# Half units for small experts, loads of the sums past a branch, and an ordered fill in a two-layer decoder with routed experts

## The chip, the cores and the metric

The kernel runs on one core of a Trainium2 chip, as one program. The metric is the device time of one execution in microseconds (us). Times shown are medians of plain runs; beside them stands one execution taken by the hardware profiler, whose records are called the trace. The engines are TensorE (PE for its matmuls, PEld for its weight loads), VectorE (DVE), ScalarE (ACT), GpSimd (POOL) and SyncE (SP), which only issues transfers here.

## What is computed

The input is `x`, 32 sequences of 100 tokens with 256 features (3200 tokens), and a context of 361 tokens with 128 features for each sequence. Six blocks follow each other, each added to its own input:

```python
x = x + _L0_attn_ref(_layernorm(x), ...)    # causal attention, 16 heads of 64
x = x + _L0_xattn_ref(_layernorm(x), ctx)   # cross attention, 16 heads of 16
x = x + _L0_ffn_ref(_layernorm(x), ...)     # 8 experts, 2 for each token, and a shared one
x = x + _L1_attn_ref(_layernorm(x), ...)    # 16 heads of 16, masked scores, no softmax
x = x + _L1_xattn_ref(_layernorm(x), ctx)   # cross attention, 16 heads of 64
x = x + _L1_ffn_ref(_layernorm(x), ...)     # 64 experts, 8 for each token, and a shared one
```

In the last block each token picks 8 of 64 experts, and an expert takes at most its first 256 tokens (`CAP`):

```python
xe = jnp.zeros((E, CAP, H)).at[sorted_e, pos].set(tok_sorted, mode='drop')
h = jax.nn.silu(jnp.einsum('ech,efh->ecf', xe, w1)) * jnp.einsum('ech,efh->ecf', xe, w3)
ye = jnp.einsum('ecf,ehf->ech', h, w2)
out = jax.ops.segment_sum(vals * flat_w[:, None], flat_t, num_segments=T)
shared = jax.nn.silu(x @ shared_gate.T) * (x @ shared_up.T) @ shared_down.T
return out + shared
```

All data is float32. With the given inputs the router uses 31 of the 64 experts, and 23 of these receive more than 128 tokens (this was worked out from the reference's routing, not from the trace).

## The kernel before, in words

The tokens lie as 25 tiles of 128 rows (`NF`), `x` stays in the on-chip memory throughout, and `xnT` holds the normed, transposed rows. The blocks run one after the other. Three things set the order of work. TensorE's order is written out by hand: inside `tc.manual_schedule` its instructions run as the program text issues them. On the other engines the framework's planner places each instruction by its inputs and its own estimate of costs, and each engine then runs its list in order, so one that waits holds those behind it. `depend` (L1696) adds an edge by hand. Lastly there are limited buffers, above all the eight PSUM banks.

**Start of layer 1's attention (`l1_attn`, L920 to L1098).** The results of layer 0's experts lie in memory as `y_d`. `gather0` (L1249) fetches the two rows that belong to each token of a tile by two indirect transfers on GpSimd (L1255, into buffers `yk`, eight of them) and adds each to `x` on VectorE (L1260). `norm_stats` (L165) takes the statistics; with the last tile of its group it adds epsilon (L182), takes the square root on ScalarE (L183) and the reciprocal on VectorE (L184). `norm_rows` then scales the rows (L187), and `norm_turn` transposes them on TensorE (L209). The groups are 4 tiles, then 3 each (`FRONT1`). `ahead` fills TensorE meanwhile with keys (`keys1`, L761) and values (`vals1`, L771) of the next block, whose inputs don't depend on `x`. Each product must be copied out of its bank by `evac` (L126), which sends every second copy to ScalarE (L130) and the rest to VectorE (L131). Before, statistics of the first four tiles stand ahead of the fill; then come four key groups (eight products) and three value halves (nine products), the turns of the first group, a fifth key group, the projections, then a fourth value half and the second group. The loop over the 32 sequences gathers the tiles of the group after next in its first three steps out of four and turns a group in the fourth; these gathers' adds have no added edge.

**Routing (`route`, `list1`, `tick`).** During the cross attention of layer 1 the router scatters each token's row, its number and its weights into `x1_d`, 256 places for each expert (L1647). `list1` (L1658) counts the rows of each expert, and lists those in use in the order of their numbers; an unused place in the list holds a dummy.

**Layer 1's experts (`l1_ffn`, L1704; `units`, L1786).** 18 pieces' worth of the shared expert run first on TensorE. A flag on GpSimd (L1760) waits for the last scattered row. Then `units` takes the first 32 listed experts, one a unit with all 256 places: `weights` (SyncE, L1794) nine units ahead, `rows` (SyncE, L1800) five ahead, `expert_turn` (transposes, L1838; copy on ScalarE, L1842), one step later `expert_hidden` (gate and up, Silu L1854, product L1856), and another step later `expert_add`: the down product, its weighting on VectorE (L1875, three buffers `ye`) and for each half of 128 rows a scatter-add on GpSimd (L1879) into one of two arrays `sum_d`, odd and even units apart. Each scatter-add waits for those of the unit two before. `room` mixes the rest of the shared expert in, at 0.9 us of it a unit from the first unit on. A branch runs units for the other 32 places if more than 32 experts are in use. At the end, SyncE loads both sums in ten transfers (L1780), VectorE adds them (L1782) and ScalarE's queue stores the output (L1783).

Of the kernel before, what the change touches and what calls it, by code (L numbers as in the profile page):

```python
# [9 lines left out]
F32 = mybir.dt.float32  # L10
# [41 lines left out]
UNITS, MORE = 32, 32  # L52
# [27 lines left out]
class Kernel:  # L80
    def __init__(self, ctx, tc, a):
# [6 lines left out]
        self.norms, self.norm_of = {}, {}  # L88
# [76 lines left out]
    def norm_stats(self, f, groups, after=None):  # L165
# [15 lines left out]
        if i == n - 1:  # L181
            nc.vector.tensor_scalar_add(rstd, mv[:, :, 1], EPS)  # L182
            nc.scalar.activation(rstd, rstd, AF.Sqrt)  # L183
            nc.vector.reciprocal(rstd, rstd)  # L184
# [576 lines left out]
    def keys1(self, n):  # L761

        b, g = divmod(n, 4)
        t = self.k1[n] = self.kv.tile([P, 2, L], F32, tag="kT", name="kT", bufs=5)
        for j in range(2):
            c = 2 * g + j
            pm = self.bank_p()[:, :L]
            self.mm(pm, [(self.w1x[1][:, c * P : (c + 1) * P], self.ctx1[b][:, :L])])
            self.evac(t[:, j, :], pm)

    def vals1(self, b, half, c):  # L771
# [7 lines left out]
        self.evac(t[:, c, :], pm)  # L779

    def l1_xattn(self):
        nc, tc, a = self.nc, self.tc, self.a
        self.route_begin()
        with ExitStack() as st:
# [100 lines left out]
            lay = Lay()  # L885
            self.xattn_stream(lay)
# [33 lines left out]
    def l1_attn(self):  # L920
        nc, tc, a = self.nc, self.tc, self.a
        with ExitStack() as st:
# [4 lines left out]
            for f in range(FRONT1[0]):  # L927
                self.gather0(pool, f)
                self.norm_stats(f, FRONT1)
# [111 lines left out]

            halves = deque((b, half) for b in range(2) for half in range(2))

            def ahead(steps, n):
                for i in steps:
                    self.keys1(i)
                for _ in range(n):
                    b, half = halves.popleft()
                    for c in range(NKC):
                        self.vals1(b, half, c)  # L1050

            with tc.manual_schedule(engines={mybir.EngineType.PE}):
                for i in range(2):
                    for f in group(i):
                        if i > 0:
                            self.gather0(pool, f, self.last_row)
                            self.norm_stats(f, FRONT1)
                    f = group(i)[0]
                    if i == 0:
                        ahead(range(4), 3)  # L1060
                    else:
                        ahead([], 1)
                    turn(f, 2)
                    turn(f + 2, len(group(i)) - 2)
                    if i == 0:
                        ahead(range(4, 5), 0)
# [4 lines left out]
                for b in range(NB + 2):  # L1071
# [12 lines left out]
                    if b0 + 8 < NB:  # L1084
                        fs = group(b0 // 4 + 2)
                        if i < 3:
                            self.gather0(pool, fs[i])
# [570 lines left out]
    def list1(self, counts):  # L1658

        nc, rp = self.nc, self.rp  # L1660
        ps = self.bank_t()[:E1, :2]
        self.mm(ps[:, 0:1], [(counts, self.ones1[:, 0:1])])
        used = rp.tile([E1, 2], F32, tag="used", name="used")
        nc.vector.tensor_single_scalar(used[:, 0:1], ps[:, 0:1], 0.0, op=ALU.is_gt)
        yield 1
        self.mm(ps[:, 1:2], [(self.before1[:E1, :E1], used[:, 0:1])])
        nc.vector.tensor_copy(used[:, 1:2], ps[:, 1:2])
        at = rp.tile([E1, E1], F32, tag="at1", name="at1")
        nc.vector.tensor_scalar(at, self.io1[:E1, :], used[:, 1:2], used[:, 0:1], ALU.is_equal, ALU.mult)
        yield 1  # L1670
        pl = self.bank_t()[:, : E1 + 1]
        self.mm(pl[:, :E1], [(self.row1, at)])
        self.mm(pl[:, E1:], [(self.ones1[:E1, :], used[:, 0:1])])
# [6 lines left out]
        nc.vector.tensor_copy(self.listi[:, 2 * E1 :], pl[:, E1:])  # L1680
# [23 lines left out]
    def l1_ffn(self):  # L1704
        nc, tc, a = self.nc, self.tc, self.a
        x = self.x
        with ExitStack() as st:
# [54 lines left out]
            end = self.units(ep, 0, UNITS, steps)  # L1762
            n = nc.values_load(self.listi[0:1, 2 * E1 : 2 * E1 + 1], min_val=0, max_val=E1)
            for u in range(UNITS, E1, MORE):
                with tc.If(n > u):
                    more = self.units(ep, u, u + MORE)

                    word = pool.tile([1, 1], F32, tag="word", name="word")
                    got = nc.sync.dma_start(word, self.sum_d[0][0:1, 0:1])
                    self.depend(got, [more.ins], "the units' sums")  # L1770
# [6 lines left out]
            for f in range(0, NF, 5):  # L1777
                at = slice(f, f + 5)
                for i in range(2):
                    got = nc.sync.dma_start(ends[i][:, at, :], sums[i][:, at, :])  # L1780
                    self.depend(got, [end.ins], "the last sums")
                    nc.vector.tensor_tensor(x[:, at, :], x[:, at, :], ends[i][:, at, :], ALU.add)  # L1782
# [3 lines left out]
    def units(self, pool, u0, u1, beside=iter(())):  # L1786

        nc, tc = self.nc, self.tc
        we, xes, xTs, hTs, added = {}, {}, {}, {}, {}

        def weights(u):
            we[u] = pool.tile([P, 768], F32, tag="we", name="we", bufs=12)
            e = nc.sync.value_load(self.listi[0:1, E1 + u : E1 + u + 1], min_val=0, max_val=E1 - 1)
            nc.sync.dma_start(we[u], self.a["wexp"][bass.ds(e, 1)].rearrange("o p n -> p (o n)"))  # L1794

        def rows(u):
            xes[u] = pool.tile([P, 2, XROW], F32, tag="xe", name="xe", bufs=8)
            e = nc.sync.value_load(self.listi[0:1, u : u + 1], min_val=0, max_val=E1)
            at = self.x1_d.rearrange("(e s p) d -> e p s d", p=P, s=2)[bass.ds(e, 1)]
            got = nc.sync.dma_start(xes[u], at.rearrange("o p s d -> p (o s) d"))  # L1800
            if u0 == 0:
                self.depend(got, [self.flag.ins], "all rows are in their places")

        with tc.manual_schedule(engines={mybir.EngineType.PE}):
            room = 0.0
            for u in range(u0, u0 + 9):
                weights(u)
            for u in range(u0, u0 + 5):
                rows(u)
            for u in range(u0, u1 + 2):  # L1810
                if u + 5 < u1:
                    rows(u + 5)
                if u + 9 < u1:
                    weights(u + 9)
                if u < u1:
                    self.expert_turn(pool, u, xes, xTs)
                if u0 <= u - 1 < u1:
                    self.expert_hidden(pool, u - 1, we[u - 1], xTs, hTs)

                room = room + 0.9 if u < u1 else 100.0  # L1820
                while room > 0:
                    took = next(beside, None)
                    if took is None:
                        break
                    room -= took
                if u0 <= u - 2:
                    self.expert_add(pool, u - 2, we.pop(u - 2), xes, hTs, added)
# [5 lines left out]
    def expert_turn(self, pool, e, xes, xTs):  # L1833
        nc = self.nc
        pt = self.bank_t().rearrange("p (k s) -> p k s", k=NK)
        for s in range(2):
            for k in range(NK):
                nc.tensor.transpose(  # L1838
                    pt[:, k, s * P : (s + 1) * P], xes[e][:, s, k * P : (k + 1) * P], self.ident
                )  # L1840
        xTs[e] = pool.tile([P, NK, CAP], F32, tag="xT", name="xT")
        nc.scalar.copy(xTs[e], pt)  # L1842

    def expert_hidden(self, pool, e, we, xTs, hTs):
        nc = self.nc
        xT = xTs.pop(e)
        ph = self.bank_s()
        for i in range(2):
            self.mm(
                ph[:, i * CAP : (i + 1) * CAP],  # L1850
                [(we[:, (2 * i + k) * P : (2 * i + k + 1) * P], xT[:, k, :]) for k in range(NK)],
            )
        g = pool.tile([P, CAP], F32, tag="ge", name="ge")
        nc.scalar.activation(g, ph[:, :CAP], AF.Silu)  # L1854
        hTs[e] = pool.tile([P, CAP], F32, tag="he", name="he")
        nc.vector.tensor_tensor(hTs[e], ph[:, CAP:], g, ALU.mult)  # L1856

    def expert_add(self, pool, e, we, xes, hTs, added):
        nc, tc = self.nc, self.tc
        xe, hT = xes.pop(e), hTs.pop(e)  # L1860
        py = self.bank_m()
        for s in range(2):
# [5 lines left out]
        one = pool.tile([P, 2, E1], F32, tag="one", name="one")  # L1868
        nc.vector.scalar_tensor_tensor(  # L1869
            one, self.mid(self.io1, 2), self.listf[:, e : e + 1], xe[:, :, D + 1 :], ALU.is_equal, ALU.mult  # L1870
        )
        by = pool.tile([P, 2], F32, tag="by", name="by")
        nc.vector.tensor_reduce(by, one, AX.X, ALU.add)  # L1873
        for s in range(2):
# [3 lines left out]
        for s in range(2):  # L1878
            got = nc.gpsimd.indirect_dma_start(  # L1879
                out=self.sum_d[e % 2][:, :],  # L1880
# [5 lines left out]
            tc.declare_no_dep(got.ins, group=f"y{e}", reason="other rows")  # L1886
            tc.add_to_no_dep_group(f"y{e}", got.ins)
            self.depend(got, added.get(e % 2, []), "the sums before")
            now.append(got.ins)
        added[e % 2] = now  # L1890
# [110 lines left out]
```

## Time and profile before

| what | time |
|---|---|
| median of 3 plain runs | 3189.18 us (3188.06 to 3191.41) |
| the profiled execution | 3172.84 us |
| its span, first to last instruction | 3171.2 us |
| mean granted TensorE clock | 0.982 |
| chain that ended last: DMA `sum<-ye,xe` | 2% of the span |
| VectorE idle ahead of L1260, for DMA `yk` | 18.1 us, 13 times |
| issue to landing of the `sum` transfers, min, median, max | 2.7, 5.1, 13.5 us |
| `xe` load (L1800), `we` load (L1794), KB each | 321 and 384 KB |

Rows of a timeline give the start, the duration, the engine, the source line, the operation, what is written from what, how many, and in brackets how long the engine stood before and what ended that. A row of a group gives the busy time, the mean in ns of one, and the idle time ahead. The line of a helper is shared by all its callers, so the tile's name tells the rows apart. `wA` and `wB` are weight tiles; `kT` and `v` with input `cT` are the fill's products. The end of a matmul is modelled, so the distance from start to start is the safer measure. A releaser is inferred: where the engine named had long been done, another was the cause.

### The profile page before, as it was taken

How to read it: one execution, taken by the hardware profiler on the slowest of the kernel's cores; microseconds unless marked ns; L12 is line 12 of the kernel's file. 1: busy time of each engine (PE TensorE's matmuls, PEld its weight loads, DVE VectorE, ACT ScalarE, POOL GpSimd, SP SyncE). 2: the span in 40 equal slices, each digit the busy share in tenths (PEclk: the TensorE clock that was granted, in tenths of full speed). 3: DMA queues.
4: the chain of work that ended last, by engine and by line, in shares of the span. 5: the costliest groups of instructions: out<-in, count | busy, mean ns of one | idle time of the engine just before them, and what ended most of it. 6: DMA issues, size and time to landing. Idle time of an engine off the chain costs nothing. (4 is left out here: it accounts for less than half of the span.)

```text
span 3171.2 us, 68007 instructions
## 1 busy us (share of the span) xinstructions
PE 3053.4 (96%) x26832; PEld 2227.2 (70%) x26832; DVE 1823.4 (57%) x4697; ACT 1397.7 (44%) x4350; POOL 927.3 (29%) x1048
## 2 busy tenths in 40 slices
PE   8999999999999999999997999999999999999993
PEld 6777777566666657888884677777777777776672
DVE  6665665566676642222226776666676666666453
ACT  5555555566656521222222225545555555455220
POOL 3222212455555443000006330011212112122474
PEclk9999999999999999999998999999999999999996
DMA  8850000000000033544552000010000000000387
GB/s 310 298 201 1 1 1 1 18 14 14 13 13 14 5 112 108 198 181 176 194 201 80 12 5 6 6 33 25 22 12 10 12 8 15 7 11 5 110 213 182
DMA packets 130105, 225.86 MB, mean 71 GB/s; under 512 B 40526, under 2 KB 108422, under 8 KB 122993
## 3 DMA queue, kind: packets, MB, share of 16 engines
q1 hardware_dynamic: 98704, 127.32, 12.5%
q0 software_dynamic: 27792, 90.81, 8.8%
q8 instruction: 215, 3.52, 0.5%
q10 hardware_dynamic: 3280, 3.28, 0.3%
q14 instruction: 114, 0.93, 0.1%
HBM read 153.77 MB, written 113.61 MB: 84 GB/s over the span
## 5 line engine op out<-in xcount | busy, mean ns | idle before, releaser
L1647 POOL DMA_INDIRECT x_d<-xr,slot x200 | 194.4, 972 | 766.3 <-DVE kT L131 241.9
L442 ACT ACTIVATE wBx<-ps_t,m 100x361 f32<-100x361 f32 x512 | 281.2, 561 | 257.7 <-DVE m L439 232.1
L612 DVE TENSOR_REDUCE m<-ps_t 100x1 f32<-100x361 f32 x512 | 240.1, 525 | 113.8 <-PE ps_t L136 113.1
L136 PE MATMUL ps_t<-xnT,wA 128*128 128x200 f32 x1536 | 299.7, 340 | 2.3 <-DMA wA<-in_wq 1.7
L439 DVE TENSOR_REDUCE m<-ps_t 100x1 f32<-100x361 f32 x512 | 241.2, 526 | 79.8 <-PE ps_t L136 76.2
L136 PEld LDWEIGHTS ps_t<-xnT,wA 128*128 128x128 f32 x1536 | 259.1, 191 | 37.8 <-issue 19.9
L136 PE MATMUL ps_t<-xT,w 128*128 128x256 f32 x1276 | 283.2, 381 | 0.7 <-ACT xT L130 0.7
L136 PEld LDWEIGHTS ps_t<-xT,w 128*128 128x128 f32 x1276 | 240.0, 190 | 41.7 <-issue 9.3
L336 POOL TENSOR_TENSOR e<-e,rz 100x400 f32<-100x400 f32 x128 | 109.5, 856 | 407.7 <-DVE rz L335 398.1
L332 ACT ACTIVATE e<-s,m 100x100 f32<-100x100 f32 x512 | 186.1, 364 | 21.4 <-DVE m L326 20.7
L136 PE MATMUL ps_t<-wA,cT 128*121 128x512 f32 x384 | 187.4, 598 | 6.6 <-DVE kT L131 5.9
L633 ACT ACTIVATE e<-ps_t 121x300 f32<-121x300 f32 x512 | 173.4, 431 | 41.7 <-PE ps_t L136 41.6
L136 PE MATMUL ps_t<-cT,wA 128*128 128x361 f32 x512 | 189.9, 495 | 1.3 <-ACTq L1246 1.3
L136 PE MATMUL ps_t<-kT,qT 64*100 64x361 f32 x1024 | 189.2, 485 | 0.9 <-ACT wBx L442 0.9
L451 PEld LDWEIGHTS ps_t<-ident,wBx 100*121 100x121 f32 x1536 | 177.8, 186 | 12.3 <-ACT wBx L442 4.8
L637 POOL TENSOR_TENSOR es<-e 121x400 f32<-121x400 f32 x128 | 132.8, 1037 | 179.8 <-ACT e L633 179.6
L136 PE MATMUL ps_t<-wA,zT 128*128 128x256 f32 x800 | 185.2, 385 | 0.0
L451 PE MATMUL ps_t<-ident,wBx 100*121 100x100 f32 x1536 | 184.9, 269 | 0.0
L1328 DVE TENSOR_TENSOR h<-ps_t,g 128x256 f32<-128x256 f32 x145 | 61.2, 424 | 199.4 <-ACT g L1327 199.4
L136 PEld LDWEIGHTS ps_t<-wA,zT 128*128 128x128 f32 x800 | 150.8, 191 | 28.2 <-ACT wBx L442 3.2
L131 DVE COPY eT<-ps_t 121x300 f32<-121x300 f32 x339 | 146.7, 461 | 30.7 <-PE ps_t L451 26.7
L469 PE MATMUL ps_z<-eT,v 121*64 121x100 f32 x3072 | 160.8, 254 | 0.0
(301 smaller groups left out, 5791.7 us busy)
## 6 DMA issues: line engine op xcount, KB each, us to landing
x_d<-fill SPq DMA_DIRECT2D x16, 1284.0 KB, 22.1
we<-in_wexp SPq DMA_DIRECT2D x32, 384.0 KB, 4.5
cT<-in_ctxT SPq DMA_DIRECT2D x64, 181.5 KB, 2.3
xe<-x_d SPq DMA_DIRECT2D x32, 321.0 KB, 4.2
xe_d<-zero SPq DMA_DIRECT2D x8, 1024.0 KB, 12.9
xe<-xe_d SPq DMA_DIRECT2D x29, 256.0 KB, 2.7
y_d<-y SPq DMA_DIRECT2D x29, 256.0 KB, 8.7
sum<-fill SPq DMA_DIRECT2D x10, 640.0 KB, 9.3
```

The lines of the kernel that those rows point to most:

```text
L131: return self.nc.vector.tensor_copy(out, in_)
L136: self.nc.tensor.matmul(out, lhsT=l, rhs=r, start=(i == 0), stop=(i == n - 1))
L332: nc.scalar.activation(t[:, i, :], s[:, i, :], AF.Exp, bias=m[:, i : i + 1], accum_out=rz[:, i : i + 1])
L336: nc.gpsimd.tensor_tensor(t[:, h, :], t[:, h, :], self.last(rz[:, h], T), ALU.mult)
L439: lay.after = nc.vector.tensor_reduce(m, ps[i], AX.X, ALU.max, negate=True)
L442: nc.scalar.activation(t[:, :L], ps[i], AF.Exp, bias=m, accum_out=sums[b][:, h : h + 1])
L451: nc.tensor.transpose(pt[:, c, :], e[n, i][:, c * KC : (c + 1) * KC], self.ident[:T, :T])
L469: nc.tensor.matmul(out, lhsT=v, rhs=eT[n, i][:, c, :], start=first, stop=last)
L612: nc.vector.tensor_reduce(m[:, j, o : o + 1], ps[r], AX.X, ALU.max, negate=True)
L633: nc.scalar.activation(t[:, r], ps[r].rearrange("p (c t) -> p c t", c=NKC), AF.Exp)
L637: nc.gpsimd.tensor_tensor(s, t[:, :, 0, :], t[:, :, 1, :], ALU.add)
L1647: got = nc.gpsimd.indirect_dma_start(out=self.x1_d[:, :], out_offset=bass.IndirectOffsetOnAxis(ap=slot[:, j, k : k + 1], axis=0), in_=xr[: ...
```

## The change

It has four parts. In `list1` the experts in use are listed in two classes: those with more than 128 rows first, then those with 1 to 128. The units become 24 whole ones and 8 of the first 128 places alone; the branch now covers the second halves of those eight and all other places, and is entered if more than 24 experts have over 128 rows or more than 32 are in use. The loads of the sums at the end are declared free of the scatter-adds inside the branch. The shared expert's remaining steps are mixed in from the fourth unit on, at 1.0 a unit. In the attention's start, all five key groups and four value halves come ahead of the first tiles' statistics, with every copy on ScalarE and the first square root behind the last copy; the adds of later gathers stand behind the rows normed last.

```diff
-UNITS, MORE = 32, 32
+WHOLE, HALF = 24, 8
+UNITS = WHOLE + HALF
...
-            nc.scalar.activation(rstd, rstd, AF.Sqrt)
+            got = nc.scalar.activation(rstd, rstd, AF.Sqrt)
+            if self.norm_after is not None:
+                self.depend(got, [self.norm_after.ins], "behind the fill's copies")
...
-            self.evac(t[:, j, :], pm)
+            self.evac(t[:, j, :], pm, self.ahead_of)
...
-        self.evac(t[:, c, :], pm)
+        return self.evac(t[:, c, :], pm, self.ahead_of)
...
+            self.ahead_of = 2
             self.xattn_stream(lay)
...
             for f in range(FRONT1[0]):
                 self.gather0(pool, f)
-                self.norm_stats(f, FRONT1)
...
+            self.ahead_of = 1
             halves = deque((b, half) for b in range(2) for half in range(2))
...
+                    if i == 0:
+                        self.norm_after = ahead(range(5), 4)
+                        for f in group(0):
+                            self.norm_stats(f, FRONT1)
+                        self.norm_after = None
                     f = group(i)[0]
-                    if i == 0:
-                        ahead(range(4), 3)
-                    else:
-                        ahead([], 1)
                     turn(f, 2)
                     turn(f + 2, len(group(i)) - 2)
-                    if i == 0:
-                        ahead(range(4, 5), 0)
...
                         if i < 3:
-                            self.gather0(pool, fs[i])
+                            self.gather0(pool, fs[i], self.last_row)
...
         nc.vector.tensor_single_scalar(used[:, 0:1], ps[:, 0:1], 0.0, op=ALU.is_gt)
+        nc.vector.tensor_single_scalar(used[:, 1:2], ps[:, 0:1], float(P), op=ALU.is_gt)
+        nc.vector.tensor_tensor(used[:, 2:3], used[:, 0:1], used[:, 1:2], ALU.subtract)
         yield 1
-        self.mm(ps[:, 1:2], [(self.before1[:E1, :E1], used[:, 0:1])])
-        nc.vector.tensor_copy(used[:, 1:2], ps[:, 1:2])
+        self.mm(ps[:, 1:3], [(self.before1[:E1, :E1], used[:, 1:3])])
+        self.mm(ps[:, 3:4], [(self.ones1[:E1, :E1], used[:, 1:2])])
+        place = rp.tile([E1, 4], F32, tag="place", name="place")
+        nc.vector.tensor_copy(place, ps)
+        nc.vector.tensor_tensor(place[:, 2:3], place[:, 2:3], place[:, 3:4], ALU.add)
+        nc.vector.tensor_tensor(place[:, 1:3], place[:, 1:3], used[:, 1:3], ALU.mult)
+        nc.vector.tensor_tensor(place[:, 0:1], place[:, 1:2], place[:, 2:3], ALU.add)
...
+        nc.vector.tensor_scalar(left[:, 0:1], pl[:, E1 : E1 + 1], float(-UNITS), 0.0, ALU.add, ALU.max)
+        nc.vector.tensor_scalar(left[:, 1:2], pl[:, E1 + 1 :], float(-WHOLE), None, ALU.add)
+        nc.vector.tensor_tensor(left[:, 0:1], left[:, 0:1], left[:, 1:2], ALU.max)
...
-            end = self.units(ep, 0, UNITS, steps)
+            whole, first, second = (0, 1), (0,), (1,)
+            units = [(u, whole) for u in range(WHOLE)] + [(u, first) for u in range(WHOLE, UNITS)]
+            end = self.units(ep, units, steps)
             n = nc.values_load(self.listi[0:1, 2 * E1 : 2 * E1 + 1], min_val=0, max_val=E1)
-            for u in range(UNITS, E1, MORE):
-                with tc.If(n > u):
-                    more = self.units(ep, u, u + MORE)
...
+            with tc.If(n > 0):
+                units = [(u, second) for u in range(WHOLE, UNITS)] + [(u, whole) for u in range(UNITS, E1)]
+                more = self.units(ep, units)
...
                     got = nc.sync.dma_start(ends[i][:, at, :], sums[i][:, at, :])
                     self.depend(got, [end.ins], "the last sums")
+                    tc.declare_no_dep(got.ins, group="behind", reason="SyncE has waited in the branch")
...
+            if len(halves) == 2:
+                at = self.x1_d.rearrange("(e s p) d -> e p s d", p=P, s=2)[bass.ds(e, 1)]
+                got = nc.sync.dma_start(t, at.rearrange("o p s d -> p (o s) d"))
+            else:
+                at = self.x1_d.rearrange("(e s p) d -> s e p d", p=P, s=2)[halves[0]][bass.ds(e, 1)]
+                got = nc.sync.dma_start(t[:, 0, :], at.rearrange("o p d -> p (o d)"))
...
-                room = room + 0.9 if u < u1 else 100.0
...
+                if beside and i > 2:
+                    room = room + 1.0 if i < n_all else 100.0
+                    while room > 0:
+                        took = next(beside, None)
+                        if took is None:
+                            break
+                        room -= took
...
+            group = f"y{u}_{halves[0]}"
+            tc.declare_no_dep(got.ins, group=group, reason="other rows")
+            tc.add_to_no_dep_group(group, got.ins)
+            self.depend(got, added.get(i % 2, []), "the sums before")
             now.append(got.ins)
-        added[e % 2] = now
+            if not beside:
+
+                tc.add_to_no_dep_group("behind", got.ins)
+        added[i % 2] = now
```

`expert_turn`, `expert_hidden` and `expert_add` take the number of halves and work on 128 or 256 columns accordingly; nothing else in them changes.

## The prediction, made before the changed kernel ran

> **What bounds the kernel now.** First the page, for the whole span.
>
> ```profile
> PE 3053.4 (96%) x26832; PEld 2227.2 (70%) x26832; DVE 1823.4 (57%) x4697; ACT 1397.7 (44%) x4350; POOL 927.3 (29%) x1048
> PEclk9999999999999999999998999999999999999996
> ```
>
> TensorE is busy for 96% of 3171.2 us. So an edit pays only where TensorE has holes, runs at a lowered clock, or has already finished. The slices show two such places, around two thirds and at the end. I asked for the stretches there (length, then busy time of PE, PEld, DVE, ACT and POOL, granted clock, DMA share, GB/s).
>
> ```profile
> 1671.00:1715.00 44.00, 29.70 (x74) 14.82 (x75) 24.40 (x65) 11.36 (x21) 30.40 (x31) 0.77 0.30 87
> 1715.00:1760.00 45.00, 38.13 (x461) 24.81 (x460) 40.33 (x118) 8.92 (x23) 32.57 (x33) 0.96 0.25 73
> 1760.00:1892.00 132.00, 131.29 (x2003) 91.78 (x2001) 97.14 (x253) 36.75 (x96) 43.34 (x50) 1.00 0.01 2
> 3006.00:3098.00 92.00, 87.44 (x449) 74.60 (x448) 48.51 (x128) 25.00 (x52) 68.26 (x45) 1.00 0.83 199
> 3098.00:3136.00 38.00, 19.20 (x88) 14.22 (x87) 13.13 (x36) 4.65 (x10) 30.91 (x21) 0.80 0.59 90
> ```
>
> The start of layer 1's attention (1671 to 1760) leaves TensorE idle for 14.3 + 6.9 = 21 us. Its clock falls to 0.77 there, so some busy time is slow as well. The timeline of the fill names the cause.
>
> ```profile
> 1688.66 3.77 PE L136 MATMUL ps_t<-wA,cT 128*121 128x512 f32 x4 [5.66 <-DVE kT L131]
> 1699.37 1.23 PE L209 MATMUL ps_t<-ident,xn 128*128 128x128 f32 x4 [6.93 <-DVE xn L187]
> ...
> 1681.93 1.28 ACT L183 ACT_TABLE_LOAD   x1
> 1690.22 0.20 ACT L183 ACTIVATE rstd<-rstd 128x4 f32<-128x4 f32 x1 [7.01 <-DVE rstd L182]
> ...
> 1696.82 0.48 DVE L1260 SCALAR_TENSOR_TENSOR x_sb<-yk,wA,x_sb 128x256 f32<-128x256 f32 x1 [6.04 <-DMA yk<-y_d,wA]
> 1698.63 0.17 DVE L184 RECIPROCAL rstd<-rstd 128x4 f32<-128x4 f32 x1
> ```
>
> These are two faults of order. ScalarE stands in the square root for 7.0 us with bank copies queued behind it, and VectorE's copies queue behind adds that wait for gathers, so TensorE runs out of PSUM banks (5.66 us). Then the reciprocal for the first tiles, whose root was ready at 1690.4, stands until 1698.63 behind an add of later tiles that waits 6.04 us for its gather.
>
> In the units stage the scatter-adds on GpSimd carry the end. The group of that line, the timeline of first and last, and the wait list of VectorE:
>
> ```profile
> L1879 POOL DMA_INDIRECT sum<-ye,xe x64 | 99.2, 1550 | 44.4 <-DVE ye L1875 29.0 <-issue 9.9 <-DVE he L1856 1.5
> ```
> ```profile
> 3006.25 1.59 POOL L1879 DMA_INDIRECT sum<-ye,xe  x1 [15.08 <-DVE ye L1875]
> ...
> 3133.17 1.55 POOL L1879 DMA_INDIRECT sum<-ye,xe  x1 [0.30 <-issue]
> 3135.99 0.09 POOL L1829 MEMSET flag_u<- 1x1 f32 x1 [1.27 <-DMA sum<-ye,xe]
> 3138.87 0.38 SPq L1780 DMA_DIRECT2D xnT<-sum  x1
> ```
> ```profile
> DVE ye L1875 <- DMA sum<-ye,xe: 28.2, 12, 4.0
> ```
>
> Each scatter holds GpSimd 1.55 us plus 0.30 us of issue, a pitch of 1.855 us. From first start to last start is 126.92 us: 63 pitches (116.9) and 10.0 us of stalls. After 3098 the pitch is unbroken, while TensorE is half idle. A further 2.88 us pass between the flag and the first load of the sums.
>
> **The change part by part.**
>
> *Ordered fill (attention).* Five key groups and four value halves (10 + 12 products, 22 copies, no DMA) now stand ahead of the first norm, with all copies on ScalarE and the root behind the last one. TensorE: two instructions of 361 columns take about 0.605 us a key product (2.4 us for the later four key instructions at half clock, 0.30 each at full), and value instructions follow at 0.43 us. From 1671.43: 10 x 0.605 + 12 x 0.857 = 16.3, so 1687.8. ScalarE keeps up: it starts at 1674.8, and 10 x 0.41 + 12 x 0.6 = 11.3 us is less than 16.3. Last copy 1688.6; table load 1.28 and root 0.20: 1690.1; reciprocal and two rows (0.19 + 0.80): 1691.1; turn at 1691.4. The gathers don't hold it: GpSimd's eight gathers are not moved, the eighth add ends at 1688.1, statistics by 1689.1. So the turn comes 8.0 us earlier than 1699.37. The two key products and three value products that now stand after it (2.4 us from 1702.67, 2.6 us from 1711.81) go ahead of it: 5.0 more. The second group (gathers 9 to 14, landed by about 1695.5 at GpSimd's 1.32 us pitch plus 2.8 us) has rows by 1699.3, just ahead of its turn. **13 us earlier at the first values product** (1715.04 to 1702).
>
> Two rules bear on this. The row has the table load at 1.28 us, with the next activation 1.30 us after a load began (2943.10, 2944.40); the Trainium skill (ScalarE: Activation LUTs, What ACT_TABLE_LOAD costs) adds a drain of about 1.38 us to a load. By the row the turn is at 1691.4, by the rule at 1692.8 and the gain 11.6; I take the row. The clock: in this trace it falls to 0.50 at about 1687.3, four us into the hole, and is whole again at 1707.9, five us after steady work began. The skill (TensorE: Matmul & The Clock Gate, Part 1) lets the clock fall only after a whole idle window of some 3.4 us. By that rule my remaining hole (1687.8 to 1691.4, 3.6 us) may pass unpunished, and the projections (6.7 us at mostly half clock) would be some 1.5 us shorter still. But here the clock also fell (0.77, 0.50) at 1735 after a stretch, 1730 to 1734, in which TensorE was busy 1.7 of 4 us. I take the row: half clock remains, no bonus.
>
> *Adds held behind the rows of the group before (attention's loop).* All 50 adds ran by 1756, with VectorE at 40.33 of 45 us and TensorE waiting 3.3 us for the masks' VectorE line and 1.8 for a copy. Now each group's adds wait for the rows of the group before. Queued behind them: on GpSimd the gathers (eight buffers), and behind those the bias adds; on VectorE nothing, since the wait is on its own order. The holes of 6.9 us can shrink, but the remaining 16 or so tiles bring about 1.55 us of VectorE each (2 x 0.48 + 0.42 + 0.17) into a stretch where it works 97 of 132 us: 97 + 25 = 122, 92%. Nothing in the trace shows that mix over 130 us; nearest is 1750 to 1760, VectorE 99% and TensorE 96.5% busy. Bounds: 6 us gained, 6 us (5% of 132) lost. I take **2 gained**, as the longest waits came from adds far ahead of need.
>
> *Half units.* The inputs, put through the reference's own routing, use 31 experts, 23 with over 128 rows. So 24 whole units hold every large one, eight half units the rest, and the branch is not entered. Scatters fall from 64 to 56: **8 x 1.855 = 14.8 us** at the unbroken pitch. TensorE saves about 1.5 us a half unit (a whole one is 3.03 us; four instructions of 128 columns follow at 0.44 us, as 3044.63 and 3045.07 show, against 0.86 for 256), off the path while GpSimd paces. The loads shrink by 8 x 160 KB, 6.5 us of transfer at 199 GB/s, also off it. A scatter waits for the one two units before: with halves that leaves 3.7 us from start, against landings of 2.7 to 13.5, median 5.1. I keep the pitch: these last experts hold at most 82 rows, and the last scatters before, started by 3133.17, had landed by 3135.99. If the median decided, a half unit would cost 2.6 us, 6 us more.
>
> *Shared expert from the fourth unit.* A hidden step (3.43 us, 3000.99 to 3004.42) leaves the path to the first addition. Turn 2994.12, hidden 2996.23 to 2997.96, turn, hidden, products of addition from 3000.1; scatter 1.83 us later as before (3004.42 to 3006.25): 3001.95, **4.3 us earlier**. The step is not gone; it now falls between additions with no backlog on GpSimd: stalls grow from 10 to 12, **2 us back**. No DMA moves with it.
>
> *Sums' loads.* Without the wait for the branch, the load follows the flag. The like pair, flag 2991.08 and load 2991.20, took 0.12 us; so 2.88 falls to 0.12, **2.7 us**. If SyncE's own branch takes that time, 0.
>
> *List.* Some six small VectorE operations (0.14 to 0.30 us each) and a few tiny products more, about 1 us. Cover: the list is ready at 2963, rows aren't sent until 2991 and weights are first used at 2996. Cost 0; 1 us without that cover.
>
> **Sum.** 13 + 2 + 14.8 + 4.3 - 2 + 2.7 = 34.8 us. The profiled execution took 3172.84 us (span 3171.2), so it would take 3138. The median of the runs shown is 3189.18, 16.3 above; I take the same saving from it: 3154. What ends last then is still GpSimd's scatters and the 32 us of loads and stores.
>
> **Rivals.**
> 1. The fill stays bound by gathers and VectorE: adds held back make a new wait in each group, and the attention gains 3 instead of 15. For: VectorE at 92%. Against: 22 copies off its path, gathers done by 1688. 3166. Chance 0.15.
> 2. Landings take over in the units: the large experts now stand in a row, so each scatter moves full rows while loads keep the DMA at 0.83; VectorE's 28.2 us of waits for buffers grow, whole units cost 0.25 us more (6), halves 2.3 instead of 1.855 (4). The units give 7 instead of 17. Against: the unbroken pitch after 3098 over mostly large experts. 3164. Chance 0.15.
> 3. The branch runs, from 25 experts over 128 rows or 33 in use: 8 second halves (14.8) and 32 whole units (64 x 1.855 = 118.7) plus a cold start of about 8, 142 us: 3296, slower than before. Against: 23 and 31. Chance 0.02.
> 4. Both stages run without the holes kept above: attention 20, units 21, load 2.7, and a little clock (1.5): 3144. Chance 0.13.
>
> The forecast has 0.55, with a range of its own of 3147 to 3162. The whole range, 3141 to 3169, takes in the rivals but the slow one and the ends. About 0.2% (6.4 us) is what a measurement of this kernel can tell from no change. Faster 0.95 (forecast, most of 1, 2 and 4), same 0.03 (both 1 and 2 together), slower 0.02.
>
> **What would show it.** First values product about 31 us after the fill's first key product (now 43.6); no root waiting ahead of copies; clock not below 0.5 for longer than some 15 us. TensorE near 100% and VectorE near 90% through the attention's loop: if TensorE falls below 97% there, the held adds cost. 56 scatters, the first about 8 us after the first unit's turn (now 12.1), first to last start about 114 us. Flag to load about 0.1 us. Wrong: more than 56 scatters, landings above 3.7 us in the half units, or a stage outside these two longer by over 3 us.

## The result and the profile after

The changed kernel takes 3165.8 us (median of four runs, 3161.37 to 3169.75) where the kernel before takes 3188.99 (3188.06 to 3191.41) in the same job: a ratio of 0.9926, 95% interval 0.9909 to 0.9943, or 23 us less. The forecast was 35 us less, and 3165.8 lies outside the range of 3147 to 3162 that it gave itself, though inside the whole range of 3141 to 3169.

The parts can't be sized from the first two profiles. The profiled execution of before took 3172.84 us, 16 below its own plain runs, and that of the changed kernel 3169.75, 4 above. So the changed kernel was profiled again in a job in which before took 3168 (experiment `e11_after`), and its profile stands beside the first one below.

The page and the stretches of the attention, first profile of the changed kernel (columns as in the prediction):

```profile
PE 3055.3 (96%) x26802; PEld 2227.6 (70%) x26802; DVE 1815.9 (57%) x4686; ACT 1400.0 (44%) x4361; POOL 915.5 (29%) x1040
```
```profile
1671.00:1715.00 44.00, 37.80 (x206) 21.13 (x208) 28.94 (x77) 19.09 (x37) 33.82 (x34) 0.84 0.29 83
1715.00:1760.00 45.00, 41.61 (x524) 27.32 (x517) 32.24 (x85) 10.67 (x27) 22.88 (x24) 0.92 0.15 42
1760.00:1892.00 132.00, 128.32 (x1838) 90.74 (x1839) 103.72 (x275) 32.51 (x88) 52.65 (x72) 1.00 0.05 14
```

TensorE does 8.1 us more in the first stretch than before and 3.5 more in the second, and 3.0 less in the third, where VectorE now also has the adds (103.7 instead of 97.1). The timeline of the fill, second profile of the changed kernel:

```profile
1684.56 1.28 ACT L185 ACT_TABLE_LOAD   x1
1685.85 0.20 ACT L185 ACTIVATE rstd<-rstd 128x4 f32<-128x4 f32 x1
1686.09 0.18 DVE L188 RECIPROCAL rstd<-rstd 128x4 f32<-128x4 f32 x1 [2.41 <-ACT rstd L185]
...
1687.04 1.98 PE L213 MATMUL ps_t<-ident,xn 128*128 128x128 f32 x8 [3.12 <-DVE xn L191]
```

Load, root, reciprocal, rows and turn follow each other without a gap; 3.1 us of TensorE's hole are left. In the units the first profile of the changed kernel has, as group of the scatters' line, as timeline of their first and last, and as a line of the wait list (total us, times, longest):

```profile
L1911 POOL DMA_INDIRECT sum<-ye,xe x56 | 86.7, 1548 | 50.7 <-DVE ye L1907 22.6 <-DMA we<-in_wexp 12.7 <-issue 6.1
```
```profile
3009.59 1.60 POOL L1911 DMA_INDIRECT sum<-ye,xe  x1 [12.67 <-DMA we<-in_wexp]
...
3132.76 1.55 POOL L1911 DMA_INDIRECT sum<-ye,xe  x1 [0.30 <-issue]
3135.55 0.09 POOL L1860 MEMSET flag_u<- 1x1 f32 x1 [1.24 <-DMA sum<-ye,xe]
3135.67 0.39 SPq L1801 DMA_DIRECT2D xnT<-sum  x1
```
```profile
DVE ye L1907 <- DMA sum<-ye,xe: 29.3, 14, 6.0
```

There are 56 scatters and the load follows the flag by 0.12 us, both as forecast. But 55 pitches of 1.855 us are 102.0, and first to last start is 123.2: 21 us of stalls, where before had 10.1.

### The profile page after: what moved, and what is told of

Same layout as the page of the kernel before. It is cut to its first block, busy times and chain, and to the rows that moved or that the text cites. A ratio compares the mean times of both kernels' runs of the same rounds, so it can differ in the third digit from the quotient of the medians.

```text
span 3167.9 us, 67935 instructions
## 1 busy us (share of the span) xinstructions
PE 3055.3 (96%) x26802; PEld 2227.6 (70%) x26802; DVE 1815.9 (57%) x4686; ACT 1400.0 (44%) x4361; POOL 915.5 (29%) x1040
## 4 chain that ended last, share of the span: by engine, by line
PE 56%; DMA 3%; DVE 2%; issue 2%; POOL 1%; SPq 1%; ACT 0%; another core or an unknown queue 0%; POOLq 0%; DVEq 0%; ACTq 0%
PE ps_t L138 37%; PE ps_t L455 5%; PE ps_z L473 5%; PE ps_t L1353 4%; DMA sum<-ye,xe 2%; PE ps_s L138 1%; PE ps_t L503 1%; PE ps_t L1016 1%; PE ps_t L1359 1%; PE ps_m L138 1%; DVE s L1006 1%; POOL sum L1911 1%; PE ps_t L213 1%; DMA wA<-sum 0%; PE ps_t L1297 0%
## 5 line engine op out<-in xcount | busy, mean ns | idle before, releaser
L336 ACT ACTIVATE e<-s,m 100x100 f32<-100x100 f32 x512 | 186.1, 364 | 20.9 <-DVE m L330 20.3
L641 POOL TENSOR_TENSOR es<-e 121x400 f32<-121x400 f32 x128 | 132.6, 1036 | 179.9 <-ACT e L637 179.7
L133 DVE COPY eT<-ps_t 121x300 f32<-121x300 f32 x339 | 146.7, 461 | 30.3 <-PE ps_t L455 26.3
```

The lines of the kernel that those rows point to most:

```text
L133: return self.nc.vector.tensor_copy(out, in_)
L336: nc.scalar.activation(t[:, i, :], s[:, i, :], AF.Exp, bias=m[:, i : i + 1], accum_out=rz[:, i : i + 1])
L641: nc.gpsimd.tensor_tensor(s, t[:, :, 0, :], t[:, :, 1, :], ALU.add)
```

## The experiments

Each ran with timed runs of the kernel before beside it on the same chip. Before took 3168 to 3171 us in all of these jobs but the last, where it took 3186. All stages below are differences of start times in each one's profile, in us. "Head" runs from the fill's first key product to the first values product, "loop" from there to the first queries of the cross attention, "start" from the first unit's turn to the first scatter, "scatters" from first to last start; "stalls" is that less 1.855 for each scatter after the first.

| kernel | ratio to before (95%) | head | loop | start | scatters (number) | stalls |
|---|---|---|---|---|---|---|
| before | 1 | 43.6 | 177.2 | 12.1 | 126.9 (64) | 10.1 |
| changed, first profile | 0.9926 (0.9909 to 0.9943) | 32.3 | 186.1 | 9.4 | 123.2 (56) | 21.1 |
| changed, `e11_after` | 0.9932 (0.9916 to 0.9947) | 30.3 | 178.5 | 9.3 | 120.0 (56) | 18.0 |
| `e1_fill` | 0.9966 (0.9953 to 0.9978) | 30.9 | 178.2 | 12.3 | 126.0 (64) | 9.1 |
| `e2_units` | 0.9966 (0.9952 to 0.9979) | 40.7 | 180.9 | 8.9 | 120.5 (56) | 18.4 |
| `e3_loop` | 0.9997 (0.9988 to 1.0005) | 54.8 | 178.0 | 8.9 | 119.5 (56) | 17.5 |
| `e4_ye` | 0.9928 (0.9915 to 0.9942) | 31.6 | 179.8 | 9.0 | 118.8 (56) | 16.8 |
| `e5_first` | 0.9916 (0.9902 to 0.9929) | 31.0 | 179.7 | 12.1 | 119.2 (56) | 17.1 |
| `e6_wait` | 0.9916 (0.9902 to 0.9930) | 31.8 | 177.5 | 8.8 | 117.6 (56) | 15.5 |
| `e7_whole` | 0.9961 (0.9947 to 0.9974) | 30.6 | 180.5 | 7.5 | 134.4 (64) | 17.6 |
| `e8_mixed` | 0.9932 (0.9919 to 0.9946) | 30.7 | 178.1 | 9.5 | 124.7 (56) | 22.6 |
| `e9_spread` | 0.9933 (0.9919 to 0.9947) | 31.4 | 177.7 | 7.6 | 120.3 (56) | 18.3 |
| `e10_none` | 0.9965 (0.9951 to 0.9978) | 32.2 | 178.6 | 7.1 | 115.9 (56) | 13.9 |
| `e12_reuse` | 0.9891 (0.9875 to 0.9908) | 31.4 | 188.0 | 9.0 | 110.2 (56) | 8.2 |

**`e1_fill` and `e2_units`: the two halves of the change.** The first is before with all edits of the attention, the second before with all the others.

> The kernel before with the ordered fill alone (keys and values ahead of the first norm, copies on ScalarE, root behind them, the loop's adds held behind the rows of the group before); units, shared expert and loads of the sums stay as before. Theory: the fill brings the first values product some 11 us forward, and the attention's loop gives about 9 of it back, because held adds spread over VectorE: loop near 186 us, saving 2 to 3, about 3186. Rival (the long loop in the changed kernel's profile was that one execution's chance): loop 177 to 179, saving 10 to 12, about 3178.

> The changed kernel with the ordered fill undone, so the list, the half units, the shared expert from the fourth unit and the loads past the branch alone. Theory: these carry nearly all of the 23 us: about 3169 (20 less than before), 56 scatters, first to last start near 120 us. Rival (the units lose to landings what they save, and the attention keeps its 11): about 3177.

Each gives 0.34%, about 10.8 us (intervals from 7 to 15). Together 21.6, which is the whole. So my theory from the first profile, that the loop gives the fill's gain back, is wrong: the head shortens by 12.7 and the loop takes 178.2. Head and loop together are the safer measure, since the loop differs by 3 us between profiles of the same attention: 220.8 and 221.6 us without the ordered fill (before, `e2_units`), 208.8 to 211.4 with it and the hold, leaving aside the two long loops.

**`e3_loop`: the adds in the loop free again.**

```
-                            self.gather0(pool, fs[i], self.last_row)
+                            self.gather0(pool, fs[i])
```

> The changed kernel with one word undone: the gathers in the loop over the sequences are free again to add as soon as they land, as before; the fill stays ordered. Theory (held adds cost the loop 9 us): loop near 177 us, about 3157. Rival (the holds do nothing, VectorE's work is the same whenever it is done): loop near 186, 3166. Second rival (without the holds the adds stand ahead of the second group's rows): the first values product comes later by up to 8 us, 3166 to 3172.

This one argument is worth 22 us: without it the changed kernel is no faster than before. The loop stays at 178.0, and the head grows to 54.8. The second rival had the right place, but three times too small. The timeline shows the mechanism:

```profile
1684.71 0.20 ACT L185 ACTIVATE rstd<-rstd 128x4 f32<-128x4 f32 x1
1691.13 0.48 DVE L1266 SCALAR_TENSOR_TENSOR x_sb<-yk,wA,x_sb 128x256 f32<-128x256 f32 x1 [7.80 <-DMA yk<-y_d,wA]
...
1704.13 0.49 DVE L1266 SCALAR_TENSOR_TENSOR x_sb<-yk,wA,x_sb 128x256 f32<-128x256 f32 x1 [0.95 <-DMA yk<-y_d,wA]
1704.53 0.17 DVE L188 RECIPROCAL rstd<-rstd 128x4 f32<-128x4 f32 x1
...
1705.36 1.14 PE L213 MATMUL ps_t<-ident,xn 128*128 128x128 f32 x4 [22.59 <-DVE xn L191]
```

The root of the first four tiles is ready at 1684.9. Its reciprocal stands on VectorE behind eight adds of later tiles, each of which waits for its gather, until 1704.5. It is the fault that the prediction read off the trace of before, only longer. Why the planner puts more adds ahead here was not tried apart (a root that comes later may be the reason). The hold keeps them behind the rows.

**`e4_ye`: four buffers instead of three for `ye`.**

```
-        y = pool.tile([P, 2, D], F32, tag="ye", name="ye", bufs=3)
+        y = pool.tile([P, 2, D], F32, tag="ye", name="ye", bufs=4)
```

> The changed kernel with four instead of three buffers for an expert's output rows (ye). Theory (VectorE's waits for a buffer, 29 us in 14 times, 2.1 each, are what delays the scatters): one buffer more gives 3.7 us of slack, stalls between scatters fall from 21 to about 12, about 3157. Rival (a scatter waits for the sums of two units before anyway, a later landing than the buffer's): the wait moves to the scatter, stalls stay near 20, 3166.

Nothing: 16.8 us of stalls, the ratio of the changed kernel. The wait moved, though not to the scatter as the rival has it: between 3006 and 3092, in the row of whole units, VectorE waits less for landed sums and more for the rows (`xe`) of the next experts. The wait lists of that stretch, first `e11_after`, then `e4_ye`:

```profile
DVE ye L1907 <- DMA sum<-ye,xe: 19.3, 7, 4.9
DVE one L1901 <- DMA xe<-x_d: 0.9, 3, 0.4
```
```profile
DVE ye L1907 <- DMA sum<-ye,xe: 4.5, 5, 1.2
DVE one L1901 <- DMA xe<-x_d: 17.1, 12, 2.7
```

The wait for a buffer is where lateness shows, not its cause.

**`e5_first`, `e6_wait`, `e7_whole`, `e8_mixed`: single parts of the units.**

```
e5_first:  -                if beside and i > 2:
           -                    room = room + 1.0 if i < n_all else 100.0
           +                if beside:
           +                    room = room + 0.9 if i < n_all else 100.0
e6_wait:   -                    tc.declare_no_dep(got.ins, group="behind", reason="SyncE has waited in the branch")
           -            if not beside:
           -                tc.add_to_no_dep_group("behind", got.ins)
e7_whole:  -WHOLE, HALF = 24, 8
           +WHOLE, HALF = 32, 0
e8_mixed:  -            units = [(u, whole) for u in range(WHOLE)] + [(u, first) for u in range(WHOLE, UNITS)]
           +            units = [p for k in range(HALF) for p in ((3 * k, whole), (3 * k + 1, whole), (3 * k + 2, whole), (WHOLE + k, first))]
```

> The changed kernel with the shared expert mixed from the first unit on at 0.9 a unit, as before. Theory: the first scatter comes 12.1 us after the first unit's turn instead of 9.0, and the hidden step that no longer falls between additions takes about 2 us of stalls away, so first to last start near 117.5: 1 us longer, about 3148 where the kernel before has 3170 on this chip. Rival (the earlier start is all gain): 3 us longer, 3150. Second rival (TensorE paces the whole units, so the place of the step doesn't matter): the same, 3147.

> The changed kernel with the loads of the sums again held for the branch's scatters. Theory: flag to first load 2.9 instead of 0.12 us, the time 2.8 longer, about 3150. Rival (SyncE's own branch takes the time): no difference, 3147.

> The changed kernel with 32 whole units and no half ones; the list still puts the experts with more than 128 tokens first. Theory: 8 scatters more at 1.855, less the 3 to 4 us for which the half units now wait for landings, 11 us longer, about 3158, with 64 scatters and 130 us from first to last start. Rival (landings and loads pace the end anyway, so the number of scatters doesn't matter): 4 us longer at most, 3151. Second rival (the prediction's full 14.8): 3162.

> The changed kernel with the same units in another order: three whole ones, then a half one, and so on, instead of all half ones last. Theory (in a row of large experts TensorE with its mixed-in work and then the transfers are the bound, and in the row of half units the landings): a half unit between gives both slack and parts the landings, first to last start falls from 119 to about 112, about 3140. Rival (the sum of work on TensorE and GpSimd is the same in any order): 3147. Second rival (a whole unit with a scatter that waits for its landing now ends last, and a half unit shortens the lead of its neighbours' transfers): 3150.

- The shared expert's later start (`e5_first` takes it back): the first scatter comes 3 us earlier with it. Stalls of the first four scatters are 0.1 us in `e5_first` and 3.8 in the changed kernel, so there it is paid back. What is left at the end can't be told: the timed ratios don't differ, while from the first unit's turn to the last scatter `e5_first` takes 131.2 us in its profile, against 126.4 to 129.3 in `e4_ye`, `e6_wait` and `e11_after`.
- The load (`e6_wait`): flag to load is 2.72 us again, and flag to end 34.8 instead of 32.4. The timed runs (interval of 4 us to each side) can't show 2.6, so this part rests on the profiles. The end of `e6_wait`:

```profile
3109.81 0.09 POOL L1859 MEMSET flag_u<- 1x1 f32 x1 [2.04 <-DMA sum<-ye,xe]
3112.53 0.39 SPq L1801 DMA_DIRECT2D xnT<-sum  x1
```

- The half units (`e7_whole` is without them): 14.4 us more from first to last start than `e11_after`, or 12.6 from the first unit's turn to the last scatter, as its first scatter comes 1.8 earlier; the time is longer by 0.3 to 0.45%, 9 to 14 us. My theory's 11 and the forecast's 14.8 are both near that and can't be told apart. The rival's 4 at most does not fit. Stalls at the end are 0.0 us between its last 15 scatters, against 3.0 between the last seven of `e11_after`. Every second half unit waits 1.2 to 1.5 us for the sums of two units before, the landings of which the rival spoke. The timeline of GpSimd, `e11_after`:

```profile
3096.70 1.54 POOL L1911 DMA_INDIRECT sum<-ye,xe  x1 [1.20 <-DMA sum<-ye,xe]
...
3101.38 1.54 POOL L1911 DMA_INDIRECT sum<-ye,xe  x1 [1.28 <-DMA sum<-ye,xe]
...
3106.27 1.54 POOL L1911 DMA_INDIRECT sum<-ye,xe  x1 [1.50 <-DMA sum<-ye,xe]
```

- Half units strewn among whole ones (`e8_mixed`): no gain, 22.6 us of stalls. The theory failed. The time, 3150.9, is that of the second rival, but its interval takes in the first rival's 3147 too; the longer stalls speak for the second, a shorter lead, which was not tried apart.

**`e9_spread`, `e10_none`, `e12_reuse`: what holds the row of whole units?** TensorE is 100% busy from 3010 to 3050, and the DMA share there is 0.95. `e9_spread` mixes the shared expert in more thinly, `e10_none` puts all but one piece of it ahead of the units, and `e12_reuse` leaves the weight loads of units 9 to 31 out, so that those units compute with other experts' weights.

```
e9_spread:  -                            yield 3.5
            +                            yield 3.5 if f + 4 <= NF else 1.2
            -                    room = room + 1.0 if i < n_all else 100.0
            +                    room = room + 0.68 if i < n_all else 100.0
e10_none:   -                while us < FIRST1 * 2.6:
            +                while us < 70.5:
e12_reuse:  +            if beside and i >= 9:
            +                we[i] = kept[i % 9]
            +                return
            ...
            +            kept[i] = we[i]
```

> The changed kernel with the shared expert mixed in at 0.68 of its cost a unit instead of 1.0, and the small last pieces counted at 1.2 instead of 3.5, so that it lasts through the half units. Theory (TensorE with mixed-in work paces the whole units at 4.2 us each instead of the scatters' 3.7, while it idles in the half units): stalls fall from 16 to about 10, 5 us shorter, 3142. Rival (transfers pace the row of large experts): stalls stay at 16, 3147. Second rival (the hidden steps themselves, 3.8 us on TensorE each, make the stalls wherever they are put): 15, 3146.

> The changed kernel with all of the shared expert but one piece ahead of the first unit, none mixed in between the units; a look at the stalls, not a better version. Theory (TensorE with mixed-in work paces scatters 0 to 44): stalls there fall from 13 to under 3, first to last start about 107, the units start about 20 us later, 3156 in all. Rival (the row of large experts is held by its transfers, whose share of time was 0.94 to 1.02 there): stalls of 8 or more remain between scatters 8 and 44, 3164 and more.

> The changed kernel without the weight loads of units 9 to 31: they use the tiles of the first nine again, so their outputs belong to other experts' weights, while every product, scatter and load of rows stays. That takes 384 KB of transfer off each of 23 units. Theory (in the row of large experts the transfers, 220 GB/s at a share of 0.95, hold the scatters' landings and the rows): landings fall to 3 or 4 us, the stalls between scatters 8 and 48 fall from 11 to 3 or fewer, the time by 8, near 3138. Rival (TensorE with the mixed-in work would make the same stalls alone): stalls between 8 and 40 stay at 8 to 10, 3145. Second rival (the landing has a time of its own that the load on the transfers doesn't change): landings stay at 5, stalls as before, 3146.

> The changed kernel once more, on the same chip as the others, for a second profile. Theory (the long attention loop, 186 us, and the long cross attention of its first profile were that execution's own): loop 177 to 180, cross attention 1049, about 23 us less than the kernel before, 3147. Rival (they belong to the kernel): loop 185, cross attention 1055 again.

The second profile of the changed kernel bears its theory out (loop 178.5 us, cross attention 1049.4, 22.5 us below before); the last section comes back to the long stages. In `e9_spread` the theory failed: 18.3 us of stalls, as the rival on transfers has it.

Two stretches of the row of whole units, first in `e10_none`, then in `e12_reuse`, then in `e11_after` (length, busy PE, PEld, DVE, ACT, POOL, clock, DMA share, GB/s):

```profile
3030.00:3050.00 20.00, 16.71 (x77) 13.30 (x76) 8.28 (x23) 4.26 (x9) 14.56 (x11) 0.91 0.97 223
3050.00:3070.00 20.00, 16.02 (x78) 12.32 (x76) 9.23 (x26) 4.85 (x10) 14.16 (x10) 1.00 0.93 222
```
```profile
3030.00:3050.00 20.00, 20.00 (x96) 16.14 (x95) 10.96 (x28) 5.13 (x12) 15.88 (x11) 1.00 0.75 135
3050.00:3070.00 20.00, 20.00 (x108) 17.67 (x108) 12.00 (x32) 5.96 (x13) 16.00 (x11) 1.00 0.88 152
```
```profile
3030.00:3050.00 20.00, 20.00 (x110) 17.75 (x109) 11.31 (x30) 5.50 (x12) 13.66 (x10) 1.00 0.95 229
3050.00:3070.00 20.00, 17.47 (x91) 14.31 (x90) 7.93 (x22) 5.12 (x11) 14.13 (x10) 1.00 0.95 222
```

All lie between scatters 8 and 48 of their kernel (in `e12_reuse` from 3031.2 on). With TensorE relieved (16 to 17 of 20 us), GpSimd still does only 14.2 to 14.6 us of scatters in 20, and 9.8 us of stalls remain between scatters 8 and 48, where `e11_after` has 11.1. My theory falls: TensorE's full row is no proof that it is the bound. The time of 3158 met its number (3156) all the same, because the units started 16 us later, not 20. With 384 KB a unit taken off the transfers, TensorE just as full, GpSimd does 15.9 to 16.0 us, close to the 16.7 that the pitch allows (20 x 1.55 / 1.855), and the stalls between 8 and 48 fall to 2.1. The time is 31.7 us below before, against 23 for the changed kernel. VectorE's waits for landed sums fall with it, `e11_after` first, then `e10_none` and `e12_reuse`:

```profile
DVE ye L1907 <- DMA sum<-ye,xe: 27.7, 12, 4.9
```
```profile
DVE ye L1907 <- DMA sum<-ye,xe: 47.2, 18, 5.2
```
```profile
DVE ye L1911 <- DMA sum<-ye,xe: 12.1, 8, 2.9
```

So the weights' transfers, which bring the traffic to 220 to 230 GB/s, make most of the stalls in the row of whole units. The DMA share alone would not have told: it is still 0.75 to 0.88 in `e12_reuse`, at 135 to 152 GB/s. Two things were not tried apart. SyncE's work of issuing these loads, 0.34 us each, went with them; but in `e11_after` SyncE stands for 51 of the 86 us from 3006 to 3092 until sums have landed, so it has time to spare. And the landings of `e12_reuse` aren't in its profile, so that part of the expectation stays open. The result fits that a buffer more, a thinner mix and another order gained nothing that can be told. No version that computes the same result is faster than the changed kernel by more than the interval.

## Why the prediction was off

Direction and place were right, and the sum was half as much again as what came (34.8 against 23). The terms, in the profiles of before and `e11_after`, whose difference from the fill to the end is 23.7 us:

| term of the sum | forecast | measured |
|---|---|---|
| ordered fill, head | 13 | 13.3 |
| adds held, loop | 2 | -1.3 |
| 8 scatters fewer | 14.8 | 14.8 |
| landings in the half units | 0 | -3.0 |
| stalls in the row of whole units (scatters 4 to 48) | 0 | -1.3 |
| shared expert: start of the scatters | 4.3 | 2.8 |
| shared expert: stalls of the first four scatters | -2 | -3.7 |
| loads of the sums | 2.7 | 2.8 |
| sum | 34.8 | 24.4 |

The cross attention and the shared expert ahead of the units, 0.9 us longer together, make up the rest, to 0.2 us. Two cautions. The 14.8 of the scatters is not measured by itself: stalls are what is left after 1.855 us for each scatter, and the test of it is `e7_whole`. And single profiles differ: kernels with these same units have 15.5 to 18.4 us of stalls on the jobs with 3168 to 3171, so the two terms of 1.3 us can't be told from nothing.

- **Fill: right, for a reason told only in half.** The head shortened as worked out. The row of the table load (1.28 us, next activation 0.01 later) was the right choice: with the drain that the Trainium skill (ScalarE: Activation LUTs, What ACT_TABLE_LOAD costs) adds, the root could not have followed the load at once. The bonus of the clock rule was rightly left out: the clock fell in the remaining hole of 3.1 us too, and the projections took 7.0 us (1689.90 to 1696.94) after 6.7 before. A stretch of `e11_after`, the granted clock third from last:

```profile
1688.00:1692.00 4.00, 3.12 (x8) 1.79 (x7) 3.71 (x9) 0.58 (x1) 3.38 (x5) 0.50 0.30 88
```

  But the held adds were costed as a small item of the loop with bounds of 6 us. They are the condition of the 13 us: without them the head takes 54.8. The price of an edge depends on what the other edits let the planner do.
- **Adds held: 2 us expected, none found.** Kernels with the hold have loops of 177.5 to 180.5, those without it 177.2 to 180.9, leaving aside the two profiles named at the end. VectorE reaches 79% between 1760 and 1892, not 92. With the head's 13.3 that makes 12.0 us for the attention, where 15 was forecast.
- **Half units: the step "I keep the pitch" failed in part.** The landings were judged by the last scatters of before, which have 7.4 us between a scatter and the one that waits for it. In half units it is 3.7, and 3.0 us were lost. The row that the prediction weighed against this (2.7, 5.1 and 13.5 us to landing) also counts the ten loads of the sums at the end; the scatters alone, as far as recorded in before (16 of 64), land after 2.7 (least), 4.3 (median) and 6.9 us. Even that median is longer than 3.7.
- **Shared expert: a step moved, not removed.** The forecast gave 2 of 4.3 us back; in the profiles the first scatter gains 2.8 and the first four stalls take 3.7 back. With no backlog on GpSimd the step stands as a stall of 2.7 us behind the fourth scatter; in `e10_none`, which has no step there, these stalls are 0.2. The 1.5 us that the start lacks go with the clock: after two waits for rows the first hidden step of `e11_after` runs at half clock, and all eight profiles with a start of 8.8 to 9.5 us have such a dip. In the three where the clock stays whole there (`e7_whole`, `e9_spread`, `e10_none`) the start is 7.1 to 7.6, where 7.8 was forecast. What decides it stays open. First `e11_after`, then `e7_whole`:

```profile
2980.00:2983.30 3.30, 2.82 (x9) 2.48 (x10) 1.32 (x5) 0.67 (x2) 0.00 (x0) 0.50 1.01 325
```
```profile
2983.10:2986.40 3.30, 3.15 (x19) 2.88 (x20) 1.43 (x6) 1.37 (x4) 0.00 (x0) 1.00 1.02 349
```

- **"The scatter-adds on GpSimd carry the end": without stalls only after 3098.** Of before's 10.1 us of stalls 9.8 lie between scatters 8 and 48. That stretch of before:

```profile
3021.40:3105.30 83.90, 78.89 (x404) 66.47 (x403) 43.06 (x115) 22.50 (x47) 61.85 (x40) 1.00 0.87 207
```

  `e12_reuse` shows for the changed kernel that the weights' transfers make most of these stalls; for before it was not tried. The profile held the hint: a share of 0.83 stood in the prediction's own row, and the loads were put down as off the path.

Rival 2 (landings take over, 3164) came within 2 us of the 3165.8, with the right mechanism for the half units (3.0 us where it had 4). For whole units it priced 6 us, and 1.3 were found; that the shared expert's stalls made up for this is luck. Rival 1 has the same number (3166) with the wrong place: the attention gave 12.0 us, not 3. Rival 4 falls with the stalls, and rival 3, the branch, did not come: there are 56 scatters.

## What to carry to other kernels

Before you cost a reordering, ask which of its edges holds the others up: take each away in thought and look at what the planner would put in the gap. When an engine paces a stage "but for some stalls", find what makes the stalls before you count what fewer instructions save or what an earlier start gains, since gains ahead of another bound can be paid back at once. A full row of TensorE next to a DMA share of 0.95 decides nothing: relieve each alone. And an operation that a new edge delays can find others put ahead of its readers on an engine that works in order, as the reciprocal did.

## What was not expected of the hardware

The same program has longer stages in some jobs. In the two jobs in which before took 3186 to 3189 us, the changed kernel's attention loop took 186.1 and 188.0 us instead of 177.5 to 180.5 with the same hold, and its cross attention 1055.7 both times instead of 1048.5 to 1049.5. In the first profile of the changed kernel two engines stand there for something that it can't name:

```profile
2935.27 0.49 ACT L507 COPY rT<-ps_t 128x400 f32<-128x400 f32 x1 [5.79 <-remote]
...
2938.32 0.57 DVE L885 TENSOR_TENSOR zT<-ps_z,rT 128x400 f32<-128x400 f32 x1 [8.52 <-remote]
```

In `e12_reuse` the same two instructions stood for 5.76 and 8.49 us; the profile of `e11_after`, from a job with 3168, and that of before show nothing of the kind there. As the ratio is the same in both kinds of job (0.9926 and 0.9932), the kernel before likely pays for it too. Its cause is open. The chip may be it: the last job ran on another chip than the jobs with 3168 to 3171, and for the first job the chip is not on record.
